# One attention-and-gating layer on one core: a new order of its ticks, and the next layer's keys in quarters

## The chip, the core and the metric

The kernel runs on one NeuronCore of a Trainium2 chip, as one program with one launch. The metric is the time of that program on the device, in microseconds (us), the median of several runs; lower is better. The engines are TensorE (PE, with its weight loads PEld), VectorE (DVE), ScalarE (ACT), GpSimd (POOL) and SyncE (SP), which here only issues transfers (DMAs). Each engine takes its instructions strictly in the order in which the program lists them, and waits where an operand or a buffer is not ready.

## The reference

Two layers over 16 batches of 512 tokens of 256 numbers, float32 throughout. Cut to what matters for this change:

```
x = x + window_attention(layernorm(x), ctx[:, :512])  # layer 0: 16 heads of 16, rotary, each query sees the 65 keys q-64..q
c = in_c                                              # layer 0, second half: a recurrence over the 16 batches
for b in range(16):
    f, i, g = sigmoid(xn@wf.T + c@uf.T + bf), sigmoid(xn@wi.T + c@ui.T + bi), tanh(xn@wc.T + c@uc.T + bc)
    c = f * c + i * g                                 # c is [512, 256], carried from batch to batch
x = x + tanh(xn @ wo.T + c @ uo.T + bo)               # the last c goes into every batch
x = x + full_attention(layernorm(x), ctx)             # layer 1: 1601 keys, 16 heads
x = x + moe(layernorm(x))                             # layer 1: 8 experts, top 2, with a capacity
```

So layer 0 must be over for all 16 batches (the last c) before layer 1 can finish anything but its keys.

## The kernel before

The kernel has three stages, one after another, each with its own pools: layer 0 (attention and recurrence), layer 1's attention with routing, and the experts. The change is in layer 0 alone, and in a helper that makes keys for layer 1.

Layer 0 puts no loop nest on the engines. It fills a list of jobs with `at(when, fn, *args)`, sorts it by `when` (ties keep the order in which they were appended, so an earlier batch comes first) and then emits job after job. `when` is counted in **ticks**, which have no length: they only set the order in which instructions stand in each engine's queue. A batch has 32 ticks, and the jobs of about three batches overlap: batch b's keys and queries are made while batch b-1's scores are taken and batch b-2's recurrence runs. In what follows ticks are given modulo 32, so that one list describes a steady batch.

The heart of layer 0 has 4 groups of heads per batch and 2 halves per group, so 8 halves of 4 ticks each:

- **scores** (L548) at ticks 0, 4, 8, ..., 28: 8 small products on row groups of PE into four PSUM tiles `s`; DVE takes a minimum with a cap out of them (L563), ACT an exponential (L564). At tick 0, 8, 16, 24 a `shift` follows: a small product (L525), copied by ACT (`nmT`, L529), that goes out to DRAM (`nm_d`, L530) and comes back as rows of `qT` (L531); the scores of the same group of heads, 8 ticks later, need them.
- **maxima** (L500) at ticks 2, 6, 10, ..., 30, for the next batch: 8 products into four tiles `s`, from which DVE takes maxima (L512).
- **values** (L578) at ticks 3.9, 7.9, ...: products with the exponentials.

All tiles `s` come from one set of 5 banks, so the maxima need three of the four banks that the scores before them used, and the other way round: PE cannot write them before DVE has read them.

Between these stand the other products, which write into a pair of banks `x`, each emptied by ACT: keys and queries (`project`, L425, then `rope` on POOL, L451 to L453, and a store), turns by PE (`turn`, L412) of the normed input (`xT`) and of the attention's normed result (`x1T`), `project_v` (L473), `out_proj` (L629), and `gate` (L657: 6 jobs of four products of 512 columns each, the costliest). `shift` uses a bank `x` as well.

Around them are the short steps that a wait can pass through. `stats` (L101, L102, on DVE) takes mean and variance of two of four row blocks of x; `norm` then has DVE add a constant (L105) and POOL do a power (L107) and four subtractions with scaling (L109). It is done twice per batch: on the input of a batch (two batches ahead) and on the attention's result (`finish`). After the attention, `recip_a`, `recip_b` take the denominators through DRAM, POOL divides (`divide`, L621), adds a bias to a fresh copy of x (`add_bias`, L405), and adds what `out_proj` made (L639, once per pair of row blocks). `step` closes the recurrence: two operations on DVE (L674, L675) and two on POOL (L676, L678).

The keys of layer 1's first batch are made in layer 0 too: `keys.load` and `keys.project` (four parts of about 400 columns), `mean`, then per half of 802 columns `fill` (POOL, L214), `add` (DVE, L221), `halve` (a store of the key, and a split in two by DVE, L158, and POOL, L161) and `store` (4 stores). Before, they stand at ticks 330 to 437 of the 480 and more, so in batches 11 to 13.

Of the kernel before, what the change touches and what calls it, by code (L numbers as in the profile page):

```python
# [12 lines left out]
F32 = mybir.dt.float32  # L13
# [3 lines left out]
ALU = mybir.AluOpType  # L17
# [4 lines left out]
P = 128  # L22
# [9 lines left out]
SKP = 1604  # L32
# [26 lines left out]
def tile_kernel(ctx: ExitStack, tc: tile.TileContext, a, out):  # L59
    nc = tc.nc  # L60
    B = out.shape[0]
# [71 lines left out]
    ke_d = [dram.tile([NG, P, SKP], F32, name=f"ke_d{i}") for i in range(2)]  # L133
# [6 lines left out]
    first_weights = [const.tile([P, 2, D], F32, name=f"{n}_w") for n in ("wk1", "wfo", "wq1")]  # L140
    wk1, wfo, wq1 = first_weights
    parts = ((0, 402), (402, 402), (804, 400), (1204, 400))
    KHALF = SKP // 2

    def stacked(t_d, m, r):
        return t_d[4 * m : 4 * m + 4].rearrange("p (h r d) n -> (p h) r d n", h=2, r=4)[:, r]

    def slotted(t_d, m):
        return t_d[2 * m : 2 * m + 2].rearrange("g (j s) n -> (g j) s n", s=32)[:, 0:HD, :]

    def key_pieces(pool, bank, bufs):
        st = {}

        def split(x, name, n):

            hi = pool.tile([P, n], F32, name=f"{name}hi", bufs=bufs.get(name, 2))
            lo = pool.tile([P, n], F32, name=f"{name}lo", bufs=bufs.get(name, 2))
            nc.vector.tensor_single_scalar(  # L158
                hi.bitcast(I32), x.bitcast(I32), -4096, op=ALU.bitwise_and
            )  # L160
            nc.gpsimd.tensor_sub(lo, x, hi)  # L161
            return hi, lo

        def mask_rows(b):
            st[b, "keep"] = pool.tile([P, SKP], F32, name="keep", bufs=1)
            nc.sync.dma_start(out=st[b, "keep"], in_=m_d[b : b + 1, :].to_broadcast([P, SKP]))

        def load(b, m, i):
            c0, n = parts[i]
            ck = pool.tile([P, 2, bufs.get("ck", S)], F32, name="ck" if "ck" in bufs else "ctxT", bufs=1 if "ck" in bufs else 2)  # L170
            nc.sync.dma_start(out=ck[:, :, 0:n], in_=a["ctxT"][b, :, :, c0 : c0 + n])
            st[b, m, i] = ck

        def project(b, m, i):

            c0, n = parts[i]
            ck = st.pop((b, m, i))
            if i == 0:
                st[b, m, "k"] = pool.tile([P, SKP], F32, name="kc", bufs=bufs.get("kc", 2))
                st[b, m, "sum"] = pool.tile([P, 4], F32, name="ksum")  # L180
            ps = bank()
            for k in range(2):
                nc.tensor.matmul(
                    ps[:, 0:n],
                    lhsT=wk1[:, k, m * P : (m + 1) * P],
                    rhs=ck[:, k, 0:n],
                    start=(k == 0),
                    stop=(k == 1),
                )
            nc.vector.tensor_tensor_reduce(  # L190
                out=st[b, m, "k"][:, c0 : c0 + n],
                in0=ps[:, 0:n],
                in1=st[b, "keep"][:, c0 : c0 + n],
                scale=1.0,
                scalar=0.0,
                op0=ALU.mult,
                op1=ALU.add,
                accum_out=st[b, m, "sum"][:, i : i + 1],
            )

        def mean(b, m):

            t = pool.tile([P, 1], F32, name="kmean")
            nc.vector.tensor_reduce(t, st.pop((b, m, "sum")), AX.X, ALU.add, negate=True)
            nc.vector.tensor_mul(t, t, rcnt[:, b : b + 1])  # L205
            st[b, m, "mean"] = t


        def half_of(h):
            return slice(h * KHALF, (h + 1) * KHALF)  # L210

        def fill(b, m, h):
            u = pool.tile([P, KHALF], F32, name="u", bufs=1)
            nc.gpsimd.tensor_scalar(  # L214
                u, st[b, "keep"][:, half_of(h)], 1.0, st[b, m, "mean"], ALU.subtract, ALU.mult
            )
            st[b, m, "u"] = u

        def add(b, m, h):
            k = st[b, m, "k"][:, half_of(h)]  # L220
            nc.vector.scalar_tensor_tensor(  # L221
                k, k, cols[:, BK1 + m : BK1 + m + 1], st.pop((b, m, "u")), ALU.add, ALU.add
            )

        def halve(b, m, h):
            k = st[b, m, "k"][:, half_of(h)]
            nc.sync.dma_start(out=slotted(ke_d[b % 2], m)[:, :, half_of(h)], in_=k)
            st[b, m, h, "halves"] = split(k, "k", KHALF)

        def store(b, m, h):  # L230
            hi, lo = st.pop((b, m, h, "halves"))
            for r, t in ((0, hi), (2, hi), (1, lo), (3, lo)):
                nc.sync.dma_start(out=stacked(ks_d[b % 2], m, r)[:, :, half_of(h)], in_=t)

        return SimpleNamespace(
            split=split,
            mask_rows=mask_rows,
            load=load,
            project=project,
            mean=mean,  # L240
            fill=fill,
            add=add,
            halve=halve,
            store=store,
        )


    with ExitStack() as l0:
# [140 lines left out]
        def at(when, fn, *args):  # L389
            jobs.append((when, len(jobs), fn, args))  # L390
# [277 lines left out]
                bias = cols[:, BG + 4 + m : BG + 5 + m]  # L668
            nc.scalar.activation(o[:, m, :], ps, AF.Tanh, bias=bias, scale=0.5 if n < 2 else 1.0)

        def step(b):
            f, i_, g_ = (state[b]["o", n] for n in range(3))
            c = state["c"]
            nc.vector.scalar_tensor_tensor(f, f, 1.0, c, ALU.add, ALU.mult)  # L674
            nc.vector.scalar_tensor_tensor(i_, i_, 1.0, g_, ALU.add, ALU.mult)  # L675
            nc.gpsimd.tensor_add(f, f, i_)  # L676
            c2 = pool.tile([P, 2, S], F32, name="c_t")
            nc.gpsimd.tensor_scalar_mul(c2, f, 0.5)  # L678
            state["c"] = c2
            del state[b]  # L680
# [6 lines left out]
        state["c"] = c_t  # L687


        T0 = 32  # L690
        for b in range(B):
            s0 = b * T0
            if b:
                at(s0 - 55 if b > 1 else -50, load, b)
            for m in range(2):
                at(s0 - 46 + 2 * m, project, b, "k", m)
                at(s0 - 43 + 2 * m, rope, b, "k", m)
                at(s0 - 42 + 2 * m, turn, "xT", b, m)
                at(s0 - 37 + 2 * m, project, b, "q", m)
                at(s0 - 34 + 2 * m, rope, b, "q", m)  # L700
                at(s0 - 15 + 4 * m, project_v, b, m)
            for p in range(2):
                at(s0 - 51 + 2 * p, stats, b, p)
            at(s0 - 48, norm, b, nc.gpsimd if b else nc.vector)
            for g in range(NG):
                at(s0 - 20 + 8 * g, slot, b, g)
                for half in range(2):
                    at(s0 - 14 + 8 * g + 4 * half, maxima, b, g, half)
                    at(s0 + 8 * g + 4 * half, scores, b, g, half)
                    at(s0 + 8 * g + 4 * half + 3.9, values, b, g, half)  # L710
                at(s0 - 8 + 8 * g, shift, b, g)
            s1 = s0 + T0

            d = 3 if b < B - 1 else 0
            at(s1 + 3, recip_a, b)
            at(s1 + 6, recip_b, b)
            at(s1 + 9.2, load_x, b)
            at(s1 + 10 + d, divide, b)
            at(s1 + 11 + d, add_bias, b)
            for p in range(2):  # L720
                at(s1 + 13 + d + 2 * p, out_proj, b, p)
            for p in range(2):
                at(s1 + 15 + d + 2 * p, stats, b, p)
            at(s1 + 17 + d, finish, b)
            for k in range(2):
                at(s1 + 21 + d + 2 * k, turn, "x1T", b, k)
            at(s1 + 24 + d, keep_xT, b)
            for n in range(3):
                for m in range(2):
                    at(s1 + 25 + d + 4 * n + 2 * m, gate, b, n, m)  # L730
            at(s1 + 36 + d, step, b)
        at(-41, lambda: fold_bias(pool, bank(), bo, BV0, wo0, RO0))
        for c in range(E * CAPP // P // 2):
            at(8 * c + 2, clear, c)
# [4 lines left out]
        for i in range(2 * NG):  # L739
            at(58 + 16 * i, constant_rows, i // NG, i % NG)  # L740

        keys = key_pieces(pool, bank, {"kc": 1, "k": 1, "ck": 402})
        at(330, keys.mask_rows, 0)
        for m in range(2):
            o = 344 + 48 * m
            for i in range(4):
                at(o + 8 * i + 1, keys.load, 0, m, i)
                at(o + 8 * i + 6, keys.project, 0, m, i)
            at(o + 32, keys.mean, 0, m)
            for h in range(2):  # L750
                at(o + 33 + 6 * h, keys.fill, 0, m, h)
                at(o + 36 + 6 * h, keys.add, 0, m, h)
                at(o + 37 + 6 * h, keys.halve, 0, m, h)
                at(o + 39 + 6 * h, keys.store, 0, m, h)
        jobs.sort(key=lambda x: (x[0], x[1]))
        for _, _, fn, args in jobs:
            fn(*args)
# [827 lines left out]
```

## Time and profile before

| | |
|---|---|
| median of 3 runs | 5900.77 us (5898.65 to 5910.45) |
| the profiled execution | 5884.69 us, span 5882.9 us |
| granted clock of PE over the span | 0.950 |
| PE, DVE, ACT, POOL busy over the span | 94%, 58%, 45%, 29% |
| layer 0: last copy of an attention tile (L587) | 1297.1 us after the start |
| one steady batch of layer 0 (batches 2 to 10), from one such copy to the next batch's | 75.4 to 78.6 us |
| batches 11, 12, 13 | 83.4, 103.7, 84.7 us |

How to read it: busy times are of instructions, so an engine can be idle for most of a wait and still show a high share over the whole kernel; what one stage costs is read from windows of that stage. A matmul is recorded in two passes here, so a product of 512 columns with two weight blocks shows as x4. The column PEclk is the clock that PE was granted, as a share of full speed. In the timeline a row begins with its start and its length in us, and a wait before it stands at the end in brackets, with what ended it.

### The profile page before, as it was taken

To read this page: it belongs to the slowest core of one execution; us is meant where nothing else is said; L and a number is where in the kernel's file an instruction comes from. 1 tells how busy PE (TensorE), PEld (TensorE's weight loads), DVE (VectorE), ACT (ScalarE), POOL (GpSimd) and SP (SyncE) were. 2 spreads that over 40 slices of the span, in tenths; PEclk is the share of its full clock that TensorE was granted. 3 is DMA by queue.
4 is the path that set the end of the run, shared out by engine and by line. 5 is a ranking of instruction groups with operands and counts; after the bars stand their busy time and mean duration, and the time that the engine had idled before them with its cause. 6 is when DMAs were issued, how large, how long until landed. Compare 5 with 4: busy or idle time off the path is not lost. (4 is left out here: it accounts for less than half of the span.)

```text
span 5882.9 us, 95873 instructions
## 1 busy us (share of the span) xinstructions
PE 5558.7 (94%) x36550; PEld 2756.8 (47%) x36550; DVE 3407.2 (58%) x9206; ACT 2636.9 (45%) x5250; POOL 1695.6 (29%) x1320
## 2 busy tenths in 40 slices
PE   7999997886999999999999999999999987999999
PEld 4555554553343343343334334334333335766776
DVE  5455554543777777777777777777777741111111
ACT  3444443430455555555555555555555551222221
POOL 3455554532122132122222212212222012222222
PEclk7889898986999999999999999999999998999999
DMA  4444334433445445445455544544544312222211
GB/s 155 148 143 131 123 119 141 138 100 108 162 164 173 163 154 200 145 165 190 160 173 170 172 169 159 186 150 164 196 158 161 112 60 78 70 79 70 65 63 46
DMA packets 353533, 806.45 MB, mean 137 GB/s; under 512 B 47405, under 2 KB 133921, under 8 KB 350898
## 3 DMA queue, kind: packets, MB, share of 16 engines
q1 hardware_dynamic: 333874, 752.25, 38.2%
q0 software_dynamic: 19200, 48.08, 2.4%
q8 instruction: 288, 4.72, 0.3%
q14 instruction: 171, 1.40, 0.1%
HBM read 479.60 MB, written 326.73 MB: 137 GB/s over the span
## 5 line engine op out<-in xcount | busy, mean ns | idle before, releaser
L975 DVE TENSOR_REDUCE pm<-m 128x1 f32<-128x402 f32 (+1 forms) x4096 | 2127.0, 570 | 622.0 <-PE m L967 599.4
L1214 ACT ACTIVATE pt<-e 128x512 f32<-128x512 f32 (+1 forms) x3328 | 1716.0, 602 | 1154.1 <-PE e L1205 1154.1
L967 PEld LDWEIGHTS m<-ks,qs 64*128 64x128 f32 x4096 | 465.6, 186 | 1368.3 <-DVE pm L975 860.0
L967 PE MATMUL m<-ks,qs 64*128 64x402 f32 (+1 forms) x4096 | 1031.2, 452 | 19.1 <-DVE pm L975 16.5
L1205 PE MATMUL e<-qe,ke 32*128 32x512 f32 x6656 | 976.3, 641 | 0.0
L1227 PE MATMUL pv<-pt,vt 128*32 128x256 f32 (+2 forms) x9656 | 976.3, 476 | 0.0
L1412 ACT ACTIVATE hT<-h,cols 128x384 f32<-128x384 f32 (+1 forms) x320 | 199.3, 623 | 753.8 <-PE h L1404 734.2
L1432 PE MATMUL y<-w,hT 128*128 128x256 f32 x2176 | 476.3, 379 | 0.0
L1404 PE MATMUL h<-xeT,w 128*128 128x384 f32 (+1 forms) x1280 | 475.6, 530 | 0.0
L1432 PEld LDWEIGHTS y<-w,hT 128*128 128x128 f32 x2176 | 410.4, 190 | 54.4
L512 DVE CUSTOM_DVE_ANT_0 tmp<-s,cst 128x192 f32<-128x192 f32 (+1 forms) x1024 | 279.0, 337 | 241.8 <-PE s L500 240.9
L563 DVE TENSOR_TENSOR pt<-s,cst 128x384 f32<-128x384 f32 (+2 forms) x768 | 248.9, 395 | 251.6 <-PE s L548 251.5
L1205 PEld LDWEIGHTS e<-qe,ke 32*128 32x128 f32 x6656 | 271.0, 179 | 259.4 <-issue 220.3
L564 ACT ACTIVATE pt<-pt 128x384 f32<-128x384 f32 (+2 forms) x768 | 246.6, 391 | 237.4 <-DVE pt L563 237.3
L1404 PEld LDWEIGHTS h<-xeT,w 128*128 128x128 f32 x1280 | 243.8, 191 | 213.5 <-issue 115.0
L1227 PEld LDWEIGHTS pv<-pt,vt 128*32 128x32 f32 (+1 forms) x9656 | 191.2, 108 | 247.1 <-issue 245.1
L1444 POOL DMA_INDIRECT out<-y_t,xe x136 | 135.1, 994 | 587.3 <-DVE y_t L1441 568.1
L1389 DVE COPY xeT<-tp 128x384 f32<-128x384 f32 (+1 forms) x80 | 45.3, 606 | 446.8 <-PE tp L1386 437.0
L1186 POOL DMA_INDIRECT slots<-row,put x128 | 133.7, 1045 | 572.8 <-issue 478.4
L214 POOL TENSOR_SCALAR u<-keep,kmean 128x802 f32<-128x802 f32 x64 | 191.7, 2995 | 265.7 <-DVE kmean L205 247.4
L1440 DVE TENSOR_TENSOR y_t<-y,b 128x256 f32<-128x256 f32 x136 | 57.7, 425 | 359.0 <-PE y L1432 359.0
L107 POOL TENSOR_TENSOR rs<-mo,mhalf 128x4 f32<-128x4 f32 x64 | 66.3, 1036 | 689.9 <-DVE mo L105 679.2
(192 smaller groups left out, 5697.3 us busy)
## 6 DMA issues: line engine op xcount, KB each, us to landing
ks<-ks_d SPq DMA_DIRECT2D x128, 802.0 KB
ks_d<-khi SPq DMA_DIRECT2D x128, 401.0 KB
ks_d<-klo SPq DMA_DIRECT2D x128, 401.0 KB
ke<-ke_d SPq DMA_DIRECT2D x64, 802.0 KB
raw_d<-raw SPq DMA_DIRECT2D x128, 256.0 KB
qs<-qs_d SPq DMA_DIRECT2D x64, 512.0 KB
ke_d<-kc SPq DMA_DIRECT2D x64, 401.0 KB
cv<-in_ctxT SPq DMA_DIRECT2D x96, 256.0 KB
```

What stands on the lines that cost most here:

```text
L214: nc.gpsimd.tensor_scalar(u, st[b, "keep"][:, half_of(h)], 1.0, st[b, m, "mean"], ALU.subtract, ALU.mult)
L512: nc.vector.tensor_tensor_reduce(out=tmp[:, lo:], in0=sc[j][:, i, lo:BW], in1=band[:, lo:], scale=1.0, scalar=NEG, op0=ALU.add, op1=ALU.ma ...
L563: nc.vector.tensor_tensor(t, sc[j][:, i, 0:w], c, ALU.min)
L564: nc.scalar.activation(t, t, AF.Exp)
L967: nc.tensor.matmul(sc[:, 0:n], lhsT=qs[r0 : r0 + 64, jp, q * P : (q + 1) * P], rhs=ks[r0 : r0 + 64, k0 : k0 + n], start=True, stop=True,)
L975: nc.vector.tensor_reduce(pms[b, g][:, q, 2 * jp + jj, part : part + 1], sc[:, 0:n], AX.X, ALU.max)
L1205: nc.tensor.matmul(sc[0:kn, :], lhsT=kt[r0 : r0 + 32, c * P : c * P + kn], rhs=qt[r0 : r0 + 32, :], start=True, stop=True,)
L1214: nc.scalar.activation(pt[0:kn, :], sc[0:kn, :], AF.Exp)
L1227: nc.tensor.matmul(pv[32 * j : 32 * j + 32, part], lhsT=vts[c // 2][0:kn, c % 2, v0 : v0 + 32], rhs=probs[b, g, c, j][0:kn, part], start=f ...
L1404: nc.tensor.matmul(ps[:, 0:n], lhsT=weights[e][0][:, k, m * P : (m + 1) * P], rhs=xeT[:, k, 0:n], start=(k == 0), stop=(k == 1),)
L1412: nc.scalar.activation(hT[:, m, 0:n], ps[:, 0:n], AF.Gelu, bias=cols[:, at : at + 1])
L1432: nc.tensor.matmul(ps[:, 0:D], lhsT=hT[:, m, t * P : (t + 1) * P], rhs=weights[e][1][:, m, :], start=(m == 0), stop=(m == NH - 1),)
```

## The change

The ticks of layer 0's jobs are set anew. Modulo 32, for a steady batch:

| job | before | after |
|---|---|---|
| gate (6) | 28, 30, 0, 2, 4, 6 | 1, 3, 5, 7, 9, 11 |
| step | 7, all at once | 12 (f times c on DVE), 14 (the rest) |
| project_v | 17, 21 | 13, 15 |
| divide, add_bias | 13, 14 | 13.5, 14.5 |
| out_proj | 16, 18 | 17, 19 |
| stats of the attention's result, finish | 18, 20; 20 | 19, 21; 22 |
| project k, rope k | 18, 20; 21, 23 | 21, 23; 23, 26 |
| turn xT | 22, 24 | 24.5, 25.5 |
| turn x1T | 24, 26 | 27, 28 |
| project q, rope q | 27, 29; 30, 0 | 29, 31; 31, 1 |

Scores, maxima, values, shift, the loads, the first stats and the first norm (16) stay where they were. After the change each gap between scores and maxima, and between maxima and the next scores, holds one such job (the two `xT` turns share one, and the two `x1T` turns stand on both sides of the values). POOL's order changes with it. Before: step, divide, add_bias, first add of `out_proj`, norm of the input, second add. After: divide, step, add_bias, norm of the input, both adds. The last batch has its own ticks, close to those before; the gates of batch 14, which stood at 508 to 518 (the last scores are at 508), stand at 513 to 523.

The keys of layer 1's first batch are made in quarters of 401 columns (`fill`, `add`, `halve`, `store` 8 times in all, where it was 4), with ticks 192 to 445: a load every 16 ticks, its product 12.5 ticks later at 13.5 or 29.5 (so beside `project_v` or the first `project q`), and a quarter every 16 ticks. In layer 1 the same helper still works in halves.

```diff
-    def key_pieces(pool, bank, bufs):
+    def key_pieces(pool, bank, bufs, pieces=2):
         st = {}
+        KN = SKP // pieces
...
         def fill(b, m, h):
-            u = pool.tile([P, KHALF], F32, name="u", bufs=1)
+            u = pool.tile([P, KN], F32, name="u", bufs=1)
...
-        def step(b):
+        def step(b, p):
             f, i_, g_ = (state[b]["o", n] for n in range(3))
             c = state["c"]
-            nc.vector.scalar_tensor_tensor(f, f, 1.0, c, ALU.add, ALU.mult)
+            if p == 0:
+                nc.vector.scalar_tensor_tensor(f, f, 1.0, c, ALU.add, ALU.mult)
+                return
             nc.vector.scalar_tensor_tensor(i_, i_, 1.0, g_, ALU.add, ALU.mult)
...
-                at(s0 - 46 + 2 * m, project, b, "k", m)
-                at(s0 - 43 + 2 * m, rope, b, "k", m)
-                at(s0 - 42 + 2 * m, turn, "xT", b, m)
-                at(s0 - 37 + 2 * m, project, b, "q", m)
-                at(s0 - 34 + 2 * m, rope, b, "q", m)
-                at(s0 - 15 + 4 * m, project_v, b, m)
+                at(s0 - 43 + 2 * m, project, b, "k", m)
+                at(s0 - 41 + 3 * m, rope, b, "k", m)
+                at(s0 - 39.5 + m, turn, "xT", b, m)
+                at(s0 - 35 + 2 * m, project, b, "q", m)
+                at(s0 - 33 + 2 * m, rope, b, "q", m)
+                at(s0 - 19 + 2 * m, project_v, b, m)
...
-            d = 3 if b < B - 1 else 0
+            last = b == B - 1
...
-            at(s1 + 10 + d, divide, b)
-            at(s1 + 11 + d, add_bias, b)
+            o = s1 + (10 if last else 13.5)
+            at(o, divide, b)
+            at(o + 1, add_bias, b)
             for p in range(2):
-                at(s1 + 13 + d + 2 * p, out_proj, b, p)
-            for p in range(2):
-                at(s1 + 15 + d + 2 * p, stats, b, p)
-            at(s1 + 17 + d, finish, b)
+                at(o + 3.5 + 2 * p, out_proj, b, p)
+                at(o + 5.5 + 2 * p, stats, b, p)
+            at(o + 8.5, finish, b)
             for k in range(2):
-                at(s1 + 21 + d + 2 * k, turn, "x1T", b, k)
-            at(s1 + 24 + d, keep_xT, b)
+                at(o + 13.5 + k, turn, "x1T", b, k)
+            at(o + 16, keep_xT, b)
+            o = s1 + (26 if last else 33)
             for n in range(3):
                 for m in range(2):
-                    at(s1 + 25 + d + 4 * n + 2 * m, gate, b, n, m)
-            at(s1 + 36 + d, step, b)
+                    at(o + 4 * n + 2 * m, gate, b, n, m)
+            for i in range(2):
+                at(o + 11 + 2 * i, step, b, i)
...
-        keys = key_pieces(pool, bank, {"kc": 1, "k": 1, "ck": 402})
-        at(330, keys.mask_rows, 0)
+        keys = key_pieces(pool, bank, {"kc": 1, "k": 1, "ck": 402}, 4)
+        at(190, keys.mask_rows, 0)
         for m in range(2):
-            o = 344 + 48 * m
+            o = 192 + 128 * m
             for i in range(4):
-                at(o + 8 * i + 1, keys.load, 0, m, i)
-                at(o + 8 * i + 6, keys.project, 0, m, i)
-            at(o + 32, keys.mean, 0, m)
-            for h in range(2):
-                at(o + 33 + 6 * h, keys.fill, 0, m, h)
-                at(o + 36 + 6 * h, keys.add, 0, m, h)
-                at(o + 37 + 6 * h, keys.halve, 0, m, h)
-                at(o + 39 + 6 * h, keys.store, 0, m, h)
+                at(o + 16 * i + 1, keys.load, 0, m, i)
+                at(o + 16 * i + 13.5, keys.project, 0, m, i)
+            at(o + 62, keys.mean, 0, m)
+            for h in range(4):
+                at(o + 64 + 16 * h, keys.fill, 0, m, h)
+                at(o + 69.5 + 16 * h, keys.add, 0, m, h)
+                at(o + 73.5 + 16 * h, keys.halve, 0, m, h)
+                at(o + 77 + 16 * h, keys.store, 0, m, h)
```

More of the change, by code (lines that the diff above doesn't have):

```diff
@@ L142, in tile_kernel @@
     parts = ((0, 402), (402, 402), (804, 400), (1204, 400))
-    KHALF = SKP // 2
     def stacked(t_d, m, r):
@@ L206, in mean, with part_of @@
             st[b, m, "mean"] = t
-        def half_of(h):
-            return slice(h * KHALF, (h + 1) * KHALF)
+        def part_of(h):
+            return slice(h * KN, (h + 1) * KN)
         def fill(b, m, h):
-            u = pool.tile([P, KHALF], F32, name="u", bufs=1)
+            u = pool.tile([P, KN], F32, name="u", bufs=1)
             nc.gpsimd.tensor_scalar(
-                u, st[b, "keep"][:, half_of(h)], 1.0, st[b, m, "mean"], ALU.subtract, ALU.mult
+                u, st[b, "keep"][:, part_of(h)], 1.0, st[b, m, "mean"], ALU.subtract, ALU.mult
             )
@@ L219, in add @@
         def add(b, m, h):
-            k = st[b, m, "k"][:, half_of(h)]
+            k = st[b, m, "k"][:, part_of(h)]
             nc.vector.scalar_tensor_tensor(
@@ L225, in halve @@
         def halve(b, m, h):
-            k = st[b, m, "k"][:, half_of(h)]
-            nc.sync.dma_start(out=slotted(ke_d[b % 2], m)[:, :, half_of(h)], in_=k)
-            st[b, m, h, "halves"] = split(k, "k", KHALF)
+            k = st[b, m, "k"][:, part_of(h)]
+            nc.sync.dma_start(out=slotted(ke_d[b % 2], m)[:, :, part_of(h)], in_=k)
+            st[b, m, h, "halves"] = split(k, "k", KN)
         def store(b, m, h):
@@ L232, in store @@
             for r, t in ((0, hi), (2, hi), (1, lo), (3, lo)):
-                nc.sync.dma_start(out=stacked(ks_d[b % 2], m, r)[:, :, half_of(h)], in_=t)
+                nc.sync.dma_start(out=stacked(ks_d[b % 2], m, r)[:, :, part_of(h)], in_=t)
         return SimpleNamespace(
```

## The prediction

> **What bounds the kernel now.** Read first: busy time by windows of one batch of layer 0 each (start:end, length, then busy PE, PEld, DVE, ACT, POOL, the granted clock, the DMA share, GB/s).
>
> ```profile
> 584.40:659.80 75.40, 69.68 (x601) 42.12 (x601) 40.22 (x202) 35.03 (x83) 39.24 (x29) 0.91 0.37 122
> ...
> 892.20:975.60 83.40, 72.21 (x613) 41.00 (x612) 42.63 (x202) 35.02 (x82) 38.62 (x27) 0.90 0.40 126
> 975.60:1079.30 103.70, 72.75 (x613) 41.20 (x613) 44.03 (x213) 34.99 (x83) 49.30 (x36) 0.82 0.42 139
> 1079.30:1164.00 84.70, 73.92 (x606) 43.13 (x606) 45.63 (x205) 35.24 (x83) 47.93 (x32) 0.90 0.47 147
> 1164.00:1233.00 69.00, 64.76 (x577) 39.96 (x576) 36.94 (x181) 25.69 (x69) 19.86 (x14) 0.85 0.38 123
> 1233.00:1297.10 64.10, 57.79 (x496) 34.38 (x495) 30.25 (x132) 24.48 (x66) 18.38 (x12) 0.84 0.25 85
> ```
>
> PE looks nearly full and nothing else is. But batches 11 to 13, with layer 1's keys, are longer at almost the same busy time; and even the PE time of a steady batch is inflated, as the timeline of PE shows.
>
> ```profile
> 601.60 0.93 PE L500 MATMUL s<-kT,qT 32*128 32x192 f32 x16
> 602.46 0.87 PE L578 MATMUL pv<-pt,v 128*32 128x128 f32 x32
> ...
> 605.80 0.48 PE L500 MATMUL s<-kT,qT 32*128 32x128 f32 x2
> 607.65 2.36 PE L500 MATMUL s<-kT,qT 32*128 32x128 f32 x14 [1.37 <-DVE pt L563]
> 609.94 1.29 PE L578 MATMUL pv<-pt,v 128*32 128x128 f32 x24
> ```
>
> The maxima (L500) take 0.93 us with other products around them, and 4.2 us (605.80 to 610.0) in the stretch that has none: there DVE must empty the tiles first. That stretch, 603.3 to 617.2, lasts 13.9 us; from 607.7 to 618 the clock is 0.5. Undisturbed, start to start, I read from PE's timeline: scores and maxima 0.76 or 0.86, values 0.69 or 0.80, shift 0.32, so 5.05 per 8 ticks and 20.2 per batch; a gate 3.63 (6: 21.8); key and query products 1.9 (4: 7.6), `project_v` 1.85 (2: 3.7), `out_proj` 1.93 (2: 3.9), turns 0.57 (4: 2.3). Sum 59.5, against a mean of 77.1 in batches 2 to 10: 17.6 us per batch are waits and half clock. That is the pool of gain.
>
> Why batch 12 took 103.7, from the timelines of SP, DVE and PE:
>
> ```profile
> 999.41 2.15 SPq L233 DMA_DIRECT2D ks_d<-khi  x2
> 1001.66 1.19 SPq L233 DMA_DIRECT2D ks_d<-klo  x2
> 1002.99 0.91 SPq L607 DMA_DIRECT2D rec_d<-den  x1
> 1015.74 1.28 SPq L612 DMA_DIRECT2D rb<-rec_d  x2
> ...
> 1028.92 0.43 DVE L101 BATCH_NORM_STATS2 st<-x_t 128x6 f32<-128x256 f32 x1 [16.08 <-DMA x_t<-in_x]
> ...
> 1030.58 3.05 PE L183 MATMUL x<-ck,wk_w 128*128 128x402 f32 x4 [17.23 <-DMA ck<-in_ctxT]
> ```
>
> The reciprocals' store stands behind 1.6 MB of key stores; SP waits 11.8 us for it, so the loads of x and of the context come late, DVE stands still before `stats`, and PE behind both.
>
> **The change, steady batch.** *Gap filling.* In each 4 ticks PE now has two other products. DVE alone needs 5.3 to 6.0 us per 4 ticks where nothing stands between (scores at 120.7, 126.0, 131.3; 72.8, 78.8, 84.6); PE needs 2.5 + 2 x 1.9 = 6.3, or 9.8 with gates. So the 9 us lost in the bare stretch go, and most of the queue of products on the two banks `x`.
>
> *What comes late instead: DVE before `stats`.* POOL's rows of today:
>
> ```profile
> 618.68 2.36 POOL L405 TENSOR_TENSOR x_t<-x_t,bo 128x1024 f32<-128x1024 f32 x1 [3.77 <-DMA x_t<-in_x]
> 621.12 1.27 POOL L639 TENSOR_TENSOR x_t<-x_t,po 128x512 f32<-128x512 f32 x1
> 623.80 1.04 POOL L107 TENSOR_TENSOR rs<-mo,mhalf 128x4 f32<-128x4 f32 x1 [1.42 <-DVE mo L105]
> 624.94 4.83 POOL L109 TENSOR_SCALAR x_n<-x_t,mo,rs 128x256 f32<-128x256 f32 x4
> 629.74 1.27 POOL L639 TENSOR_TENSOR x_t<-x_t,po 128x512 f32<-128x512 f32 x1
> ...
> 631.04 0.43 DVE L101 BATCH_NORM_STATS2 st<-x_t 128x6 f32<-128x256 f32 x1 [1.80 <-POOL x_t L639]
> ```
>
> Here only the second add stands behind the norm, and DVE waits 1.8 us. After the change both adds stand behind `step`, `add_bias` and the norm. Count from the scores of tick 12 on PE (0). DVE begins them 0.9 later (651.27 to 652.18 today) and needs 1.94, `stats` 1.1, the step's second operation 1.22: 5.1. Then maxima 14 (2.2), `stats` 1.1: 8.45; scores 16 (1.94): 10.4; maxima 18, which PE ends at 10.7: 12.7. POOL starts at 5.1: 2.36 + 2.78 + 2.36 + 1.04 + 4.83 + 1.27 (rows L676, L678, L405, L107, L109, L639) with small gaps: 20.0. So DVE waits 7.3 us before `stats` 19, with scores 20 and maxima 22 behind it. PE still has `out_proj`, values, scores 20 and a key product (to 16.0), then needs `s` tiles: maxima 22 end at 23.2 instead of 16.8. **Loss 6.4.**
>
> *Smaller ones.* Scores 16 wait for late maxima 14: 0.6. In ticks 24 to 28 the second `xT` turn needs the bank of `shift`, which ACT copies after the exponentials: 2.0 (today 1.45 at 643.69, up to 2.1). POOL's norm of the result then ends at 30.4, the first `rope` k at 34.2; SP stands before its store and issues the `nm_d` row behind it at 36, lands it and loads it by about 41, while PE wants scores 32 at 39.2: 1.8 (between 0 and 6). Half clock: 13.7 us of each batch today, much of it while PE waits anyway; the new hold is long enough to bring it again, and a key product, values and turns behind it would take twice as long (v 3.78 instead of 1.99 at 160.0): 3.5, between 0 and 7. `step` split in two: nothing, DVE has over 3 us between maxima 10 and scores 12.
>
> Sum: 59.5 + 6.4 + 0.6 + 2.0 + 1.8 + 3.5 = 73.8, so 3.3 us a batch, **12 batches (2 to 13): -40** (range 67 to 79 per batch: -120 to +23).
>
> [...]
>
> **The keys.** Before: 271.8 - 3 x 77.1 = 40.5 us in batches 11 to 13. After, over batches 6 to 13: 8 products of 1.6 (1076.25 to 1077.79) = 12.8, half of them at 13.5, where PE waits for DVE anyway: 6.4. POOL's `u` at 1.5 (half of 2.997, L214), 4 of 8 between the norm and the adds, in the chain that holds DVE: 6. DVE: 8 x (0.66 + 0.65 + 0.32) = 13, half exposed: 6. Stores of 0.2 MB at ticks 13 and 29, away from the reciprocals (6): 4 for lateness, between 0 and 10; rows of 1604 bytes and 20 more issues on SP cost nothing unless SP is what is late (then 20 x 0.6 = 12). Sum 22, **gain 18** (8 to 25).
>
> **The ends.** Batch 1 took 75.5 with two gates; it has none after, but bare stretches (3 x 5.6, then 41 as above, with 7 for half clock and mask work): 65, **-10**. Batch 14: 69 to 64, **-5**. Batch 15 has its gates on the scores and maxima it still has: 64 to 56, **-8**. Tail: gates of batch 14 move behind the last scores (26.4 us after them instead of 18.9), but the divide today waits for POOL's step until 1317.6 although its operand was there near 1309.5, and now goes ahead; the step falls between the adds instead. The norm ends 43.9 us after the last scores today (1291.2 to 1335.1), and then after 26.4 + 1.9 (product) + 0.6 (copy) + 1.3 + 5.1 (step) + 1.3 + 1.1 + 6.0 = 43.7: **0** (-3 to +6). Layer 1 and the experts: unchanged, they begin on the last c.
>
> **Total:** -40 - 18 - 10 - 5 - 8 = -81. The profiled execution (5884.69) becomes 5804; it stood 16 us under the median, so the median becomes **5820**.
>
> **Rivals.**
> 1. *PE becomes the bound.* POOL is through early, DVE does not wait, the clock stays: 67 a batch, -121 - 41: 5738. For it: PE's need exceeds DVE's in every slot. Against it: nothing lets the adds pass `step` and the norm. 15%.
> 2. *The steady batches gain nothing.* [...] For it: half clock has outlasted a wait by 11 us (busy from 1112, 0.5 until 1123.4). 20%.
> 3. *Slower: SP's order.* A late `rope` holds SP, behind it the `nm_d` row; scores 32 wait each batch, ACT's exponentials too. It decides from 80.5 us a batch (41/12 over 77.1), which is 6.7 above my sum: scores 32 waiting over 8 us. At 83: +71 - 41: 5930. For it: SP waited for `rope` up to 9.6 us, 17 times in batches 3 to 10, but then scores 32 came 23 us after scores 24, now 13. Against: POOL has 39 us of work a batch. 8%.
>
> Forecast itself: 57%.
>
> **Numbers.** Range 5750 to 5890: it holds the forecast (5775 to 5865 alone), rival 2 and a third of rival 1, and leaves out the rest of it and rival 3 (about 18%). 0.2% (12 us) is what a measurement here can tell: faster than 5889: 86%; within: 6%; slower: 8%.
>
> **What would show it.** Batch windows of 72 to 76 us, none over 85. In PE's timeline no maxima of over 3 us except those of tick 22; DVE's `stats` waiting about 7 us for POOL's add (L639) once a batch; `u` eight times in layer 0 at about 1.5 us; SP's wait for the `rec_d` store under 4 us. Wrong if DVE does not wait there (rival 1), if the clock is under 0.85 in the batch windows (2), or if scores wait for `nm_d` (3).

## The result

The changed kernel takes 5850.46 us (median of 5 runs, 5844.44 to 5856.85) against 5898.65 for the kernel before (5 runs): a ratio of 0.9923, 95% interval 0.9902 to 0.9944, so 48 us faster. Forecast were 5820 and 81 us: the direction, and the range of 5750 to 5890, held; the size was 33 us too large. The profiled execution took 5856.85 us (span 5855.0).

Layer 0 ends (last copy of an attention tile) at 1242.2 us instead of 1297.1. The batch windows of the changed kernel (start:end, length, busy PE, PEld, DVE, ACT, POOL, clock, DMA share, GB/s), a plain batch (5) first, then batches 12, 14 and 15:

```profile
419.60:494.90 75.30, 66.77 (x601) 37.95 (x600) 39.96 (x197) 34.53 (x84) 39.37 (x30) 0.93 0.47 149
955.80:1035.90 80.10, 65.20 (x601) 37.72 (x600) 41.71 (x202) 34.41 (x84) 45.85 (x35) 0.90 0.40 130
1117.10:1179.00 61.90, 60.77 (x561) 36.57 (x560) 35.23 (x181) 25.49 (x68) 20.39 (x14) 0.87 0.42 137
1179.00:1242.20 63.20, 55.93 (x493) 32.86 (x493) 29.82 (x130) 24.68 (x65) 18.41 (x12) 0.86 0.26 86
```

The batch of 103.7 us is gone (80.1 in its place). A plain batch, though, is hardly shorter than before: 75.3, where 73.8 was forecast. Its timeline on PE shows where most of its 15.8 us over the bare work of 59.5 are:

```profile
463.85 1.98 PE L425 MATMUL x<-ctxT,wk 128*128 128x512 f32 x4
465.76 0.59 PE L500 MATMUL s<-kT,qT 32*128 32x192 f32 x2
470.53 2.56 PE L500 MATMUL s<-kT,qT 32*128 32x192 f32 x14 [4.18 <-DVE pt L563]
473.03 3.78 PE L425 MATMUL x<-ctxT,wk 128*128 128x512 f32 x4
476.74 1.24 PE L578 MATMUL pv<-pt,v 128*32 128x128 f32 x32
...
479.13 0.63 PE L412 MATMUL x<-cst,x_n 128*128 128x128 f32 x4
481.65 0.66 PE L412 MATMUL x<-cst,x_n 128*128 128x128 f32 x4 [1.89 <-ACT nmT L529]
...
492.01 0.39 PE L525 MATMUL x<-cst,nm 128*16 128x128 f32 x2
494.30 3.49 PE L657 MATMUL x<-x1T,gates 128*128 128x512 f32 x4 [1.89 <-ACT rot L438]
497.58 2.12 PE L657 MATMUL x<-c_t,gates 128*128 128x512 f32 x4
```

Maxima 22 begin at 465.76 and the next product at 473.03, 7.3 us for 0.86. The key product behind them takes 3.78 us instead of 1.98, at half clock. The second turn waits for the bank of `shift`, and the first gate waits for ACT, again with a product at half clock behind it. Who holds DVE, and through it the maxima, stands in the timelines of POOL and DVE:

```profile
454.08 2.38 POOL L678 TENSOR_TENSOR gate<-gate,gate 128x1024 f32<-128x1024 f32 x1 [10.15 <-DVE gate L677]
456.55 2.78 POOL L680 TENSOR_SCALAR c_t<-gate 128x1024 f32<-128x1024 f32 x1
459.30 2.36 POOL L405 TENSOR_TENSOR x_t<-x_t,bo 128x1024 f32<-128x1024 f32 x1
461.61 1.04 POOL L107 TENSOR_TENSOR rs<-mo,mhalf 128x4 f32<-128x4 f32 x1
462.76 4.85 POOL L109 TENSOR_SCALAR x_n<-x_t,mo,rs 128x256 f32<-128x256 f32 x4
467.56 2.49 POOL L639 TENSOR_TENSOR x_t<-x_t,po 128x512 f32<-128x512 f32 x2
...
468.87 0.43 DVE L101 BATCH_NORM_STATS2 st<-x_t 128x6 f32<-128x256 f32 x1 [6.27 <-POOL x_t L639]
```

POOL works without a gap from 454.08 to 468.8 through step, bias and norm before the add that `stats` needs, the chain that the prediction added up. Just before, it stood idle for 10.15 us until DVE's half of `step` was done: POOL is not short of time, its work comes in the wrong place.

### The profile page after: what moved, and what is told of

Its sections match the earlier page's. It is cut to its first block, busy times and chain, and to the rows that moved or that the text cites. A ratio compares the mean times of both kernels' runs of the same rounds, so it can differ in the third digit from the quotient of the medians.

```text
span 5855.0 us, 95951 instructions
## 1 busy us (share of the span) xinstructions
PE 5518.5 (94%) x36550; PEld 2706.0 (46%) x36550; DVE 3405.4 (58%) x9214; ACT 2629.4 (45%) x5250; POOL 1699.5 (29%) x1328
## 5 line engine op out<-in xcount | busy, mean ns | idle before, releaser
L214 POOL TENSOR_SCALAR u<-keep,kmean 128x802 f32<-128x802 f32 (+1 forms) x68 | 193.1, 2839 | 268.9 <-DVE kmean L205 250.3
```

The costliest lines, as they stand in the source:

```text
L214: nc.gpsimd.tensor_scalar(u, st[b, "keep"][:, part_of(h)], 1.0, st[b, m, "mean"], ALU.subtract, ALU.mult)
```

## The experiments

The theory: two things were won. The key stores no longer stand in front of the reciprocals' store, and the bare stretch is filled; but in a plain batch most of what the second gives is handed back to POOL's order, with half clock and ACT's wait behind it. The rival: the hand-over of the `s` banks between DVE and PE, and the clock, set a batch, and the hold merely stands in front of them. Batch windows below are means over batches 2 to 5 unless said. Each comparison with the changed kernel uses its second set of runs, or, for `rot_buffers`, `step_late` and `norm_early`, medians on a chip where the kernel before took nearly the same (5891.46 against 5891.87).

**Each half of the change alone.** `ticks_alone` keeps the new ticks and takes the old key block back:

```diff
-        keys = key_pieces(pool, bank, {"kc": 1, "k": 1, "ck": 402}, 4)
-        at(190, keys.mask_rows, 0)
+        keys = key_pieces(pool, bank, {"kc": 1, "k": 1, "ck": 402})
+        at(330, keys.mask_rows, 0)
...
```

> The new ticks with the keys of layer 1 as before (halves, ticks 330 to 437). By the batch windows of after (batches 2 to 5: 75.7 us against 77.6; batches 14 and 15: 8 less; batch 1: 5 less) the ticks alone give 25 to 35 us: 5865 to 5875, and batch 12 is long again (95 to 105). If the whole gain comes from the keys, it takes 5890 to 5900.

`keys_alone` is the old order of ticks with the new key block and the helper in quarters.

> The old ticks with the keys in quarters at ticks 192 to 445. Batches 11 to 13 were 40 us over a plain batch, and the keys of after seem to cost 18 over eight batches: 20 to 25 us faster than before, 5874 to 5879, no batch over 85. If the ticks make the room that the quarters need, the keys still hold a batch up and the gain is under 10.

Measured: `ticks_alone` 5851.49 us, ratio to before 0.9931 (0.9919 to 0.9944), 40 us; `keys_alone` 5867.9, ratio 0.9958 (0.9943 to 0.9973), 24 us, and when it was run again (below) 15 us. The sum is more than the whole, 52 us on that chip: with the new ticks in place, the keys bring only 12 more (5851.49 to 5839.91). `ticks_alone` still has the long batch, in its windows and on SP, with the reciprocals' store behind the key stores; `keys_alone` has 77.1 there:

```profile
947.80:1049.10 101.30, 78.57 (x614) 44.77 (x613) 43.11 (x207) 34.27 (x84) 48.23 (x35) 0.83 0.46 148
```

```profile
972.81 1.66 SPq L233 DMA_DIRECT2D ks_d<-khi  x2
974.57 2.08 SPq L233 DMA_DIRECT2D ks_d<-klo  x2
976.75 0.80 SPq L607 DMA_DIRECT2D rec_d<-den  x1
988.43 1.25 SPq L612 DMA_DIRECT2D rb<-rec_d  x2
```

```profile
970.40:1047.50 77.10, 70.72 (x601) 42.58 (x600) 42.44 (x204) 35.01 (x82) 45.26 (x34) 0.91 0.42 136
```

The longest wait of SP for that store (`rb<-rec_d` behind `rec_d<-den`) is 10.8 us in `ticks_alone`, as it was 11.8 before, and 4.7 in `keys_alone`. So each half works without the other. Whether the smaller pieces or their places in the order free the reciprocals was not separated: `keys_alone` changes both. The ticks gave a little more than expected (40 against 25 to 35), spread thinly: 3 us in batch 0, 2 in batch 1, 1.8 a batch in batches 2 to 10, 10 in batches 11 to 13, 3 to 9 at the end.

**POOL's order undone.** `norm_and_step_moved` makes all the moves below; `step_late` only the last line (the second half of `step`), `norm_early` only the first three (load, stats and norm of the input).

```diff
-                at(s0 - 55 if b > 1 else -50, load, b)
+                at(s0 - 63 if b > 1 else -50, load, b)
-                at(s0 - 51 + 2 * p, stats, b, p)
+                at(s0 - (59 if b > 1 else 51) + 2 * p, stats, b, p)
-            at(s0 - 48, norm, b, nc.gpsimd if b else nc.vector)
+            at(s0 - (56 if b > 1 else 48), norm, b, nc.gpsimd if b else nc.vector)
...
-                at(o + 11 + 2 * i, step, b, i)
+                at(o + 11 + (14.5 if b < B - 2 else 2) * i, step, b, i)
```

> After, with the load, stats and norm of the input 8 ticks earlier (ticks 1, 5, 7, 8) and the step's second half at 26.5, behind the ropes: POOL then has nothing but add_bias before the two adds. Theory (POOL's order holds DVE before stats, and half clock and ACT's wait for rot follow from that hold): the 6.3 us wait is gone, maxima 22 take under 3 us, batches 2 to 5 take 66 to 69 instead of 75.7, 90 to 120 us less than after: 5730 to 5760. Rival (the hand-over of the s banks between DVE and PE and the clock set a batch, and the hold only stands in front of them): 73 to 76 a batch, 5830 to 5850.

> After, with only the step's second half moved from tick 14 to 26.5: POOL's chain before the adds is 5.1 us shorter, but the norm of the input still stands before them and can't begin before DVE's L105 at tick 16. Theory: DVE's wait before stats 19 falls from 6.3 to 3 to 5 us, batches 2 to 5 take 72 to 75; 10 to 40 us less than after (5840 to 5850 there). If the norm is not what holds, the wait is under 1.5 us and a batch under 71.

> After, with only the load, stats and norm of the input 8 ticks earlier, the step's second half at 14 as in after: POOL has step (5.1) and add_bias (2.4) before the adds, so DVE waits 1 to 2 us before stats 19, batches 2 to 5 take 69 to 71, 60 to 80 us less than after: 5765 to 5785, near the 5760 of both moves. If the step is the larger part of the hold, DVE still waits over 3 us and the gain is under 40.

Plain batches and waits here are those of batches 2 to 5:

| | median us | less than the changed kernel | plain batch us | DVE's wait for the add, us |
|---|---|---|---|---|
| changed kernel again | 5839.91 | | 75.5 | 4.5 to 6.0 |
| `step_late` | 5803.37 | 37 | 72.2 | 1.7 to 2.4 |
| `norm_early` | 5771.44 | 68 | 68.9 | none to 0.4 |
| `norm_and_step_moved` | 5760.59 | 79 | 69.0 | none |

One row of DVE with such a wait, in `step_late`:

```profile
379.85 0.43 DVE L101 BATCH_NORM_STATS2 st<-x_t 128x6 f32<-128x256 f32 x1 [2.38 <-POOL x_t L639]
```

These waits of `step_late` are shorter than the 3 to 5 us expected, and those of `norm_early` than the 1 to 2. From batch 6 on, with key work among the rest, they are longer: 4.4 to 6.2 us in `step_late`, 1.0 to 2.6 in `norm_early`; with both moves none is left before batch 15. That is where both moves gain their 11 us over `norm_early`, not in the plain batch.

With both moves the windows of two batches, then POOL:

```profile
396.40:465.90 69.50, 64.04 (x601) 36.66 (x600) 40.45 (x197) 34.25 (x83) 40.69 (x30) 0.95 0.53 161
465.90:535.70 69.80, 63.84 (x610) 36.63 (x609) 41.36 (x201) 34.51 (x84) 40.95 (x30) 1.00 0.49 157
```

```profile
429.89 2.37 POOL L405 TENSOR_TENSOR x_t<-x_t,bo 128x1024 f32<-128x1024 f32 x1 [0.78 <-DMA x_t<-in_x]
437.12 1.27 POOL L639 TENSOR_TENSOR x_t<-x_t,po 128x512 f32<-128x512 f32 x1 [4.87 <-ACT po L637]
440.93 1.27 POOL L639 TENSOR_TENSOR x_t<-x_t,po 128x512 f32<-128x512 f32 x1 [2.54 <-ACT po L637]
```

POOL now waits for the adds' operands instead of coming late. The hold is gone: 6.5 us a batch by moving the load, the stats and the norm of the input and half of `step`, none of which does less. The rival falls. The norm is the larger part; the step alone gives half, and with the norm gone the step's 5 us nearly fit in, since the adds must wait for their operands anyhow. The stats move along with the norm, so two of DVE's own steps (about 1.2 us each, at 407.76 and 411.53 in `norm_early`) also leave the place before the hold; that share was not measured apart.

The two things that the theory put behind the hold behave otherwise. Half clock falls from 10.7 us a batch to 2.6 with both moves, but only to 7.5 in `norm_early`, whose plain batch is just as short. There 3.2 us less at half speed explain at most 1.6 of the 6.6 us gained. And the first gate's wait for ACT does not go with the hold: over three batches it is 6.9 us in the changed kernel and 10.2 with both moves. Of the expected 90 to 120 us, 79 came: a plain batch is at the upper end of 66 to 69, and batches with keys are still at 70 to 72. This version, 0.9782 of the time before (0.9769 to 0.9795), is the best that was found.

**The gate's wait for ACT.** `rot_buffers` is the changed kernel with two more buffers each for the key and query products that POOL turns.

```diff
-            r = pool.tile([P, S], F32, name="r")
+            r = pool.tile([P, S], F32, name="r", bufs=4)
...
-            rot = pool.tile([P, S], F32, name="rot")
+            rot = pool.tile([P, S], F32, name="rot", bufs=4)
```

> After, with 4 instead of 2 buffers for r and rot, so that ACT does not wait for the stores of the keys before it empties the bank of the second query product: the 1.8 us wait of the first gate and the half clock behind it (1.7) go, 3 us a batch, 30 to 45 us less than after: 5795 to 5815. If that wait only follows from the hold of DVE, the gates wait for something else at the same place and nothing changes (within 10 us).

Measured: 5834.24 us, 6 less than the changed kernel, which is within the spread (the two medians of the changed kernel differ by 10.6). The waits of PE from 268 to 495 us, about batches 3 to 5 (total, times, longest), first of the changed kernel:

```profile
PE x L657 <- ACT rot L438: 6.9, 4, 2.6
...
PE s L500 <- DMA qT<-q_d: 3.1, 4, 1.3
```

and with the buffers:

```profile
PE s L500 <- DMA qT<-q_d: 11.1, 6, 3.0
...
PE x L657 <- ACT rot L438: 0.7, 3, 0.2
```

The wait went as meant, and another took its place: the maxima now wait for the loads of queries, which stand in SP's queue behind the same stores (`k_d<-r` at 486.73, `qT<-q_d` at 488.96 there). The 30 to 45 us were wrong: with the first of two waits behind one late queue taken away, PE stood at the second.

**The turns.** `moves_and_turn` adds to `norm_and_step_moved` a later tick for the second `xT` turn, `moves_turn_rot` also the buffers of `rot_buffers`.

```diff
-                at(s0 - 39.5 + m, turn, "xT", b, m)
+                at(s0 - 39.5 + 2 * m, turn, "xT", b, m)
```

> As norm_and_step_moved, and the second xT turn at tick 26.5 instead of 25.5, so that it finds the bank of shift already copied. In the timeline of norm_and_step_moved the two turns take 3.3 us for 1.14 and half clock follows. Theory: 2 to 3 us a batch less, 66 to 67, 5725 to 5740. If maxima 26 then wait as long for DVE (which begins scores 24 0.9 us after PE and needs 1.94), at most 1 us a batch: 5745 to 5760.

> As moves_and_turn, with 4 buffers for r and rot. In norm_and_step_moved the first gate still waits 2 us for ACT behind the stores of the keys, with half clock behind it. If that wait goes here without the loads of kT and qT taking its place as they did in rot_buffers: 3 us a batch, 40 us less than moves_and_turn, near 5690. If they do: 0 to 10 us less.

Measured: 5775.05 and 5774.19 us, on a chip where the kernel before took 5889.9: ratios 0.9804 (0.9787 to 0.9820) and 0.9798 (0.9782 to 0.9814), no better than without (0.9782); layer 0 ends at 1163 us in both, against 1154.9. PE does reach the end of the turns sooner, and then stands elsewhere (timeline of PE, then of SP, `moves_and_turn`):

```profile
454.91 0.87 PE L578 MATMUL pv<-pt,v 128*32 128x128 f32 x32
458.15 1.66 PE L548 MATMUL s<-qT,kT 32*128 32x192 f32 x16 [2.38 <-DMA qT<-nm_d]
459.75 0.61 PE L525 MATMUL x<-cst,nm 128*16 128x128 f32 x2
462.80 3.78 PE L657 MATMUL x<-x1T,gates 128*128 128x512 f32 x4 [2.44 <-ACT rot L438]
```

```profile
451.81 1.27 SPq L457 DMA_DIRECT2D k_d<-r  x2
453.13 0.45 SPq L588 DMA_DIRECT2D raw_d<-raw  x1
453.69 0.37 SPq L530 DMA_DIRECT2D nm_d<-nmT  x1
456.13 0.54 SPq L531 DMA_DIRECT2D qT<-nm_d  x1
```

This is the mechanism of the third rival: the `nm_d` row is issued behind the store of the turned keys, lands, is loaded, and scores 32 wait for it. The waits of PE over three batches show the exchange, first `norm_and_step_moved`, then `moves_and_turn`:

```profile
PE x L412 <- ACT nmT L529: 5.3, 3, 1.8
...
PE s L548 <- DMA qT<-nm_d: 0.2, 1, 0.2
```

```profile
PE s L548 <- DMA qT<-nm_d: 7.5, 3, 2.8
PE x L412 <- ACT nmT L529: 1.6, 3, 0.6
```

In the changed kernel the wait for `nm_d` does not show up at all; that this is because PE comes late there itself is argued from this exchange. The buffers of `moves_turn_rot` again only move a wait: the gates no longer wait for ACT, and the maxima wait 10.3 us for `qT<-q_d` instead of 1.6, the second case of its expectation.

**What spreads between executions.** The changed kernel, the kernel before and `keys_alone` were each run and profiled a second time.

> The changed kernel unaltered, for a second trace: in the first traces layer 0 ended 52 us earlier than before but the program only 28, so layer 1's attention took about 24 us longer, though its code is the same. If that is a spread between executions, the end of layer 0 is again at 1242 to 1245 and layer 1's 16 batches differ from the first trace by 10 to 30 us; if the change slows layer 1, they are the same to within 5 us.

> The kernel before unaltered, for a second trace: batches 1 to 5 took 77.2 us on average in the first trace, but 75.3 with keys_alone, whose instructions are the same there. If that is a spread between executions (half clock 15.4 against 10.2 us a batch), this trace lies anywhere from 75 to 78; then the new ticks gain nothing in a plain batch (75.7). If it is again 77 or more, they gain 1.5 to 2 us.

> keys_alone unaltered, for a second trace. Up to tick 190 it issues what before issues, but its batches 1 to 5 took 75.3 us where before took 77.2 and 76.9 in two traces. If the difference is a spread between executions, this trace shows 75 to 78 there and half clock of 10 to 17 us a batch; if it is fixed (the key tiles are smaller, so other tiles lie elsewhere in SBUF), it shows 75.3 again.

`after_again`: 5839.91 us, ratio 0.9912 (0.9898 to 0.9927); layer 0 ends at 1237.4. From the end of layer 1's first batch to that of its last it took 3139.5 us, and 3148.8 in the first trace; the kernel before took 3128.4 and 3139.1, so the two kernels are 20 us apart there in the first pair of traces and level in the second. Layer 0 ended 54.9 us earlier in the first pair (the expectation has 52) and 56.7 in the second, and from its end to the program's end the changed kernel took 27 us longer in the first pair and 1.5 in the second. What the first pair seemed to give back in layer 1 is for the most part a spread between executions, and the medians (48 and 52 us) come near layer 0's gain.

`before_again`: layer 0 ends at 1294.1, a plain batch (2 to 5) takes 77.1 us, and the long batch is there again:

```profile
353.30:431.30 78.00, 71.49 (x601) 42.83 (x600) 39.88 (x200) 35.04 (x82) 39.31 (x29) 0.89 0.49 150
980.00:1083.70 103.70, 72.93 (x613) 41.55 (x612) 43.97 (x212) 35.01 (x82) 49.33 (x36) 0.82 0.42 139
```

`keys_alone_again`: 5874.74 us, ratio 0.9971 (0.9956 to 0.9986), 15 us instead of the 24 of the first time; batches 1 to 5 take 75.4 us, as in its first trace (75.3), against 77.2 and 76.9 in the two of the kernel before. Up to tick 190 all engines get the same instructions, so the 1.7 us between the means are not the ticks, and with two traces of each that agree within 0.3 hardly a chance spread. What differs most is half clock around the turns: from values 24 to values 28 `keys_alone` takes 8.4 us in seven of these ten batches, the kernel before 9.5 to 11.5 in nine of ten. Why it falls there in one kernel and not in the other is open; other places of the tiles were not tried. In `keys_alone` these are 8.5 us gained in batches 1 to 5, before its first key is made, out of its 15 to 24. It also matters for what the ticks gain: against `keys_alone` (75.1 and 75.3 in batches 2 to 5) the changed kernel's plain batch (75.7 and 75.5) gains nothing, while `ticks_alone` (76.0) gains about 1.4 over the kernel before (77.6 and 77.1).

## Why the prediction was right, and where it was off

The terms against two traces of each kernel (means, in us):

| term | forecast | measured |
|---|---|---|
| plain batch, before and after | 77.1 to 73.8 | 77.3 to 75.6 |
| 12 plain batches | -40 | -20 |
| keys: over plain batches, before and after | 40.5 to 22 | 40 to 18.5 |
| batch 0 | 0 | -4 |
| batch 1 | -10 | -4 |
| batch 14 | -5 | -5 |
| batch 15 | -8 | 0 |
| tail: last scores to the norm's end | 0 | 0 |

The measured terms add up to 55 us; layer 0 ended 55 and 57 us earlier. Of the 33 us between the 81 forecast and the 48 measured, the plain batches are 20, batch 15 is 8 and batch 1 is 6; the keys (3.5 more than forecast) and batch 0 (4) went the other way. The time alone does not tell forecast from rivals: 5850 lies in the forecast's own 5775 to 5865 and nearer to rival 2's 5860 (the keys and the ends alone, 41 us) than to 5820. What tells them apart is the hold, which was there as worked out, and the clock, which stayed at 0.88 or more in batches 2 to 13 of both traces where rival 2 asked for under 0.85. One sign failed: batches with key work took up to 81.2 us, not 72 to 76.

*The hold* was right in place, cause and size: maxima 22 lose 6.4 us (465.76 to 473.03 for 0.86) where 6.4 were worked out, DVE waits 6.3 where 7.3 were, and the moves of step and norm show that the order before the add is the cause.

*The term that was mis-sized is the plain batch's smaller waits and half clock.* Scores 16 (0.7 against 0.6) and the second turn (2.0 against 2.0) were right. Half clock took 3.9 us (key product, values, gate) against 3.5. The 1.8 us of scores 32 behind the `nm_d` row did not come; in the same place the first gate waited 1.8 us for ACT, which stands behind the stores of the keys: the right queue, another victim. Maxima 18 waited 0.6 for their queries, which the sum left out. For the batch of 419.6 to 494.9 that makes 59.5 + 15.4 = 74.9 of its 75.3, against 59.5 + 14.3; the mean of the plain batches is 75.6, so 0.7 are in none of these rows. The missing 1.6 us of gain a batch are small beside the 17.6 of waits that the change worked on, but 12 batches make 20 us of them: the forecast of the gain was a small difference of two large sums.

*The turns and the clock.* In the batch shown all four turns, 479.1 to 484.9, take 0.63 and 0.66 us, at a granted clock of 1.00 (479 to 485). In the kernel before, half clock began at 638.5, within the second turn (1.01 us from 638.29), after PE had waited 1.91 us for ACT in front of the first turn at 636.93. Without the hold, half clock began among the four turns in 6 of batches 2 to 8 of `norm_early` and in 4 of them in `norm_and_step_moved` (a turn of 1.11 us at 453.3), each time with a wait of about 1.8 us for the bank of `shift` in front of the second turn. In `moves_and_turn` and `moves_turn_rot`, where that wait is 0.6 us at most, it began there in none of 14 batches, with the same turns in 4.9 us. The changed kernel has the wait too (1.89 us in the batch shown), and half clock among the turns in 3 of 14 batches. So in the changed kernel and these four runs half clock among the turns came only with that wait, and not always with it; what else decides was not shown. The clock records of the first traces of the two kernels hold 0.5 and 1.0 alone (66 of each before, 64 of each after). The key product took 1.98 us at 1.0 and 3.78 at 0.5, and the gate at 494.30, with 0.5 from 494.6 on, 3.49.

*The keys* were right in mechanism and near in size (18.5 against 22 over the plain batches); SP's longest wait for the reciprocals' store fell from 11.8 to 5.4 us (forecast: under 4). `u` took 1.66 us on average, eight times (forecast: about 1.5), and in the four batches where it stands in POOL's chain DVE's wait for the add grew to 8.4 or 8.5 us. *Batch 15* was over-rated: without key and query products its turns come straight behind the norm and wait for each of its four parts. *The tail* came out as worked out: the norm ends 44.0 us after the last scores begin (1236.4 to 1280.4), 43.7 in the second trace.

Rival 1 (PE as the bound, 67 a batch) was the right picture of what is behind the hold: 69.0 when it is taken away. Rival 2 (nothing gained in a plain batch) was as near as the forecast: -20 lies halfway between its 0 and -40. Its evidence, half clock until 1123.4 with PE "busy from 1112", is weaker than the prediction took it: PE waited 0.65 us before 1112.12 and 0.75 before 1114.09.

## What to carry to other kernels

Filling every gap of the fullest engine with one job each also orders the queues of all the others; add up, for each short step that another engine waits for, what now stands before it in its own in-order queue. Here a norm and half of a `step`, on an engine that is busy half of the time, held the whole batch, and moving them 8 and 12.5 ticks (the norm with its load and stats) was worth more than the change itself, 79 us against 52. A burst of stores belongs away from any transfer whose landing the issuing queue waits for (11.8 and 10.8 us with the burst in front, 4.7 and 5.4 without). And a wait behind a late queue was not removed here by more buffers for the first who waited.

## What the runs showed that was not expected

- Two kernels with the same instructions up to tick 190 differ there by 1.7 us in 76, twice each, mostly through where half clock falls.
- The granted clock does not set a plain batch here. At nearly the same work the mean over batches 2 to 5 is 0.90 before, 0.93 after the change and 0.98 with both moves; but `norm_early` at 0.95 is as short (68.9 us) as both moves at 0.98 (69.0), and `keys_alone` has 0.93 in the old order.
- Without the hold, half clock begins among the turns in 10 of 14 batches where one turn waits about 1.8 us, and in none of 14 where it waits 0.6 at most.
- The third rival's wait, absent from the changed kernel, appears (2.4 us) once PE is quicker through the turns.
